# A two-layer graph transformer on one core: layer 0 gets its own order of token blocks, with the 20-token tile in its first block

## The chip, the cores and the metric

The kernel runs on one core of one Trainium2 chip. The metric is the time of one launch in device microseconds, as the median over several runs. A profile is taken from one execution of its own; its span runs from the first to the last instruction.

## The reference

Two layers of the same kind run one after the other over 2708 tokens of 512 features, in float32. A token attends only to its neighbours in a sparse graph (and itself), with 8 heads of 64.

```python
mask = adj.astype(jnp.float32) + jnp.eye(n, dtype=jnp.float32)
q = (h @ Wq.T + bq).reshape(n, N_HEADS, D_K)      # k and v alike
scores = jnp.einsum('nhd,mhd->hnm', q, k) / jnp.sqrt(jnp.float32(D_K))
scores = jnp.where(mask[None, :, :] == 0, jnp.float32(-1000000000.0), scores)
attn = jax.nn.softmax(scores, axis=-1)
ctx = jnp.einsum('hnm,mhd->nhd', attn, v).reshape(n, D_MODEL)
h1 = _layer_norm(h + ctx @ Wo.T + bo, ln1_g, ln1_b)
ff = jax.nn.relu(h1 @ W1.T + b1) @ W2.T + b2      # D_FF = 2048
h2 = _layer_norm(h1 + ff, ln2_g, ln2_b)
```

The graph is random: a pair of tokens is joined with a probability of some 0.003, so a token has 9 neighbours or so, and few have over 20.

## The kernel before, in words

**Tiles and lists.** The kernel first makes a list of neighbours for every token, sorts the tokens by their number of neighbours, and cuts the sorted row into 22 tiles (NT) of 128 tokens; the last, tile 21, has 20. `CAPS` (L37) gives the number of neighbours that a tile's tokens may have: 22 for tile 0, then 14, 13, 12, 12, 11, 11, 10, 10, 9, 9, 9, 9, 8, 8, 8, 7, 7, 7 for tiles 1 to 18, 6 and 5 for 19 and 20, and 3 for tile 21. Keys and values of all tokens lie in DRAM (`kv_d`), queries too (`q_d`); rows are gathered by index.

**Attention** (`attend`, L1759, class `Tile`, L1139) runs on VectorE and ScalarE. It takes a tile's neighbours in chunks of one or two (`SLOTS`). For a chunk, `weights` multiplies the gathered keys by the query and sums over each head on VectorE (L1150, L1156); `weigh` takes the exponential on ScalarE (L1169), weighs the values on ScalarE (L1176) and VectorE (L1182), and adds them up on VectorE (L1189). After a tile's last chunk, `sums` (L1193) forms the sums, and `divided` (L1215, L1220) writes the attended rows `cx` on ScalarE. `weigh` comes one step behind `weights`, `sums` two and `divided` three, so that the next tile's first chunks stand between a tile's last chunk and its cx. Gathers run three chunks ahead (`EARLY`) into five buffers (`KVB`).

**Blocks.** The rest of a layer goes by blocks of two tiles (L1754), eleven in all: `attended` (L1434) turns cx with four transposes (tp, L1293), projects it (o, L620; L615 for the 20-token tile, whose four parts of the sum run side by side on quarters of the array and are added by VectorE in L630), adds the input and normalizes; `feed_forward` (L1475) has for each of 16 slices f of 128 hidden features four matmuls of the first product (pf, L1523), a relu on ScalarE (ft, L1534) and the slice's part of the second product (a, L1496, L1511 for the 20-token tile); `keys_values` (L1709) makes keys and values for the next layer, inside the next block's f = 5 to 8.

**Seven products.** In layer 0, most pairs of full tiles use `feed_forward_by_seven` (L1613): two slices f and two tiles make a 2x2 product of blocks, which is done with seven matmuls of 128x256 (L1643) in place of four of 128x512, with sums of weights (forms) and sums of activations. The weights' sums are formed once, on VectorE, in block 1 (`form`, L1587) and stored in DRAM (`form_d`); each block fetches them again, 21 times 128 KB, into three places (`ask_forms`, L1605), on SP's queue. The places lie in the buffer of Wq (`prepared`, L1575). The last pair of slices, f = 14 and 15, stays ordinary (L1673, L1677). One form overwrites a piece of W2, and the last block in seven products loads it again (`form_back`). After the products, VectorE puts the parts together (L1695 to L1703).

**The order of the work** is written out by hand: each engine runs its instructions in the order of the program. The main loop (L1928) goes through the blocks and, inside, through f. After a slice's matmuls, `advance` (L1820) lets the attention go on by a number of steps that the paces (L51 to L61) give for this f; a step of two neighbours costs 1.0, and what is left over is kept, up to 1.5. `until` (L1832) takes as many steps as a tile's cx needs. Block k+1 is attended inside block k: in layer 0 its first tile at f = 10 and its second at f = 11 (12 and 13 in block 0).

**Before block 0**, in layer 0, `first_queries` (L990) makes all queries in order of tokens, and stores them. Since the stored queries are complete only at the end, the first three tiles of the order have queries of their own (`own`, L1022); the fourth tile's query is gathered from `q_d` once all are stored (`asked`, L1122). Block 0's tiles are attended and turned in between.

**The seam of the layers.** In layer 0's last block (L1997 to L2009), which is the 20-token tile with tile 0 and ordinary, the next layer's W1, W2, Wq and Wo come in on SP's queue, with the stored activations of the next layer's first eight tiles. Then the queries of layer 1 run (L2016 and L1887 to L1923), with the last block's keys and values in between; the attention of layer 1 begins when the last keys are stored.

Both layers have one order: (20, 19), (18, 17), (8, 9), (7, 10), (6, 11), (5, 12), (4, 13), (3, 14), (2, 15), (1, 16), (21, 0).

## Time and profile before

| | before |
|---|---|
| median of 3 runs | 1831.61 us (1830.18 to 1831.98) |
| the profiled execution: span | 1827.1 us |
| what lies around the span, against the median | 4.5 us |
| mean granted TensorE clock | 0.999 |
| layer 0, block 0 starts | 250.12 us |
| layer 0, block 1 starts | 314.95 us |
| layer 0, block 2 starts (seven products) | 393.74 us |
| layer 0, last block starts | 1003.91 us |
| layer 1, block 0 starts | 1142.47 us |

A page gives the busy time of each engine: PE is TensorE's matmuls, PEld its weight loads, DVE VectorE, ACT ScalarE, POOL GpSimd, and SP the queue that issues most loads. A timeline's row has the start, the length, the engine, the line, what is written <- what is read, the shape and the number of instructions that were merged (a float32 matmul shows as two records), and in brackets the idle time ahead of it with its releaser. The names are the program's: pf and ft are the first product and its relu, a and c the sums of the second product, tp a transpose, cx a tile's attended rows, o, q, k and v the projections.

### The profile page before, as it was taken

The numbers are of one execution on the slowest core, as the hardware profiler recorded it, in microseconds if no ns is written. First come the engines' busy times: TensorE is split into PE (matmuls) and PEld (weight loads), VectorE is DVE, ScalarE is ACT, GpSimd is POOL, SyncE is SP. The second block draws the span as 40 slices with busy tenths as digits, with TensorE's granted clock in tenths as the row PEclk, the third lists the DMA queues.
The fourth block names the chain that finished last, engine by engine and source line by source line (L and its number), as shares of the span: only waits on it lengthen the run. The fifth ranks groups of instructions, "written<-read, shape, count | busy, mean of one in ns | idle before, by whom it ended". The sixth has DMA issues, their size and how long they took to land.

```text
span 1827.1 us, 22528 instructions
## 1 busy us (share of the span) xinstructions
PE 1807.5 (99%) x6563; PEld 1162.6 (64%) x6563; DVE 1457.5 (80%) x2447; ACT 949.1 (52%) x3271; POOL 798.9 (44%) x745
## 2 busy tenths in 40 slices
PE   9999999999999999999999999999999999999998
PEld 4444456666777867778677644666666666666666
DVE  5887778988989889898895257887898888889853
ACT  5771435645556545564543213665665565567531
POOL 3334755534455544454430042353464555456302
PEclk9999999999999999999999999999999999999999
DMA  9997987757576676765652876745564664555300
GB/s 340 369 335 256 371 283 245 236 169 241 195 255 228 197 236 196 219 233 181 228 191 70 287 257 248 285 160 180 178 228 150 228 224 169 195 197 194 133 14 21
DMA packets 158061, 393.80 MB, mean 216 GB/s; under 512 B 17514, under 2 KB 60894, under 8 KB 157928
## 3 DMA queue, kind: packets, MB, share of 16 engines
q0 software_dynamic: 70608, 252.12, 40.2%
q1 hardware_dynamic: 77162, 118.55, 18.7%
q10 hardware_dynamic: 10158, 21.61, 3.1%
q8 instruction: 53, 0.87, 0.2%
q14 instruction: 80, 0.66, 0.1%
HBM read 338.78 MB, written 53.44 MB: 215 GB/s over the span
## 4 chain that ended last, share of the span: by engine, by line
PE 89%; DVE 5%; issue 2%; ACT 2%; DMA 1%; POOL 1%; POOLq 0%; SPq 0%; DVEq 0%
PE pf L1523 18%; PE a L1496 17%; PE pf L1653 9%; PE k L620 8%; PE v L620 8%; PE q L620 8%; PE o L620 8%; PE c L1643 4%; PE a L1643 3%; PE tp L1293 2%; DVE sc L1156 1%; DVE kv L1150 1%; DMA forms<-form_d 1%; PE a L1677 1%; PE a L1673 1%
## 5 line engine op out<-in xcount | busy, mean ns | idle before, releaser
L1113 POOL DMA_INDIRECT kv<-kv_d,listed x420 | 524.0, 1248 | 291.2 <-DVE acc L1189 133.9
L1523 PE MATMUL pf<-hT,w 128*128 128x256 f32 (+1 forms) x1792 | 393.2, 367 | 0.1
L1523 PEld LDWEIGHTS pf<-hT,w 128*128 128x128 f32 x1792 | 323.5, 190 | 103.1 <-issue 64.4
L1496 PE MATMUL a<-w,ft 128*128 128x512 f32 x800 | 373.1, 592 | 0.0
L1176 ACT ACTIVATE kv<-kv,p 128x64 f32<-128x64 f32 x1232 | 311.0, 335 | 5.0
L1275 POOL TENSOR_TENSOR rd<-va,mhalf 128x1 f32<-128x1 f32 (+1 forms) x88 | 80.5, 914 | 520.6 <-DVE va L1273 520.5
L1150 DVE TENSOR_TENSOR kv<-kv,q 128x1024 f32<-128x1024 f32 (+1 forms) x222 | 256.9, 1157 | 13.3 <-DMA q<-q_d,ident_i 10.9
L1156 DVE TENSOR_REDUCE sc<-kv 128x16 f32<-128x1024 f32 (+1 forms) x222 | 257.9, 1162 | 7.6
L1189 DVE TENSOR_TENSOR acc<-acc,kv 128x1024 f32<-128x1024 f32 (+2 forms) x178 | 205.4, 1154 | 37.6 <-ACT kv L1176 23.0
L1653 PE MATMUL pf<-hT,w 128*128 128x256 f32 x1024 | 233.1, 379 | 1.6 <-ACT ft L1664 1.6
L1496 PEld LDWEIGHTS a<-w,ft 128*128 128x128 f32 x800 | 150.1, 190 | 113.2 <-issue 101.3
L1653 PEld LDWEIGHTS pf<-hT,w 128*128 128x128 f32 x1024 | 193.9, 190 | 35.4 <-issue 7.9
L1534 ACT ACTIVATE ft<-pf,b 128x256 f32<-128x256 f32 (+1 forms) x208 | 95.0, 459 | 197.6 <-PE pf L1523 195.2
L1169 ACT ACTIVATE p<-sc,listed 128x8 f32<-128x8 f32 x420 | 104.0, 296 | 147.2 <-DVE sc L1156 135.7
L620 PE MATMUL o<-wo,cT 128*128 128x512 f32 x336 | 151.0, 593 | 1.0 <-ACT cT L1298 1.0
L1664 ACT ACTIVATE ft<-pf,b 128x256 f32<-128x256 f32 x96 | 44.9, 468 | 160.5 <-PE pf L1653 160.5
L1182 DVE TENSOR_TENSOR kv<-kv,p 128x512 f32<-128x512 f32 (+1 forms) x178 | 123.4, 693 | 4.5 <-ACT p L1169 4.3
L620 PEld LDWEIGHTS o<-wo,cT 128*128 128x128 f32 x336 | 63.4, 190 | 74.7 <-issue 65.5
L745 DVE MAX8 tops<-code 128x8 f32<-128x247 f32 (+2 forms) x242 | 78.6, 400 | 28.3 <-ACT code L740 28.3
L1281 DVE SCALAR_TENSOR_TENSOR h<-h,rd,ln_b 128x512 f32<-128x512 f32 (+1 forms) x88 | 65.9, 749 | 39.5 <-POOL rd L1275 39.5
L1220 ACT ACTIVATE cx<-acc,su 128x64 f32<-128x64 f32 (+1 forms) x352 | 88.2, 333 | 12.9 <-DVE su L1212 7.4
L1455 DVE TENSOR_TENSOR h<-o,xb 128x512 f32<-128x512 f32 (+1 forms) x44 | 30.3, 688 | 80.0 <-PE o L620 65.0
(232 smaller groups left out, 2323.5 us busy)
## 6 DMA issues: line engine op xcount, KB each, us to landing
aj<-in_adj SPq DMA_DIRECT2D x42, 677.0 KB, 6.3
forms<-form_d SPq DMA_DIRECT2D x168, 128.0 KB, 4.2
kv_d<-kvs ACTq DMA_DIRECT2D x21, 512.0 KB, 5.5
xg<-in_xT SPq DMA_DIRECT2D x19, 512.0 KB, 7.4
w<-in_W SPq DMA_DIRECT2D x16, 512.0 KB, 6.2
kv<-kv_d,listed POOLq DMA_INDIRECT x420, 6.3
zT_d<-zT SPq DMA_DIRECT2D x22, 256.0 KB, 5.1
xb_d<-h SPq DMA_DIRECT2D x21, 256.0 KB, 5.7
```

The source lines that it names most:

```text
L620: nc.tensor.matmul(o[:r], xs(c), wm[:, c, :], start=(c == 0), stop=(c == NC - 1))
L1113: return nc.gpsimd.indirect_dma_start(out=to, out_offset=None, in_=table[:, :], in_offset=bass.IndirectOffsetOnAxis(ap=s, axis=0), bounds_ ...
L1150: nc.vector.tensor_tensor(kv[:r, :c, :DM], kv[:r, :c, :DM], self.q[:r].unsqueeze(1).to_broadcast([r, c, DM]), ALU.mult,)
L1156: nc.vector.tensor_reduce(self.sc[:r, s0 : s0 + c, :], kv[:r, :c, :DM].rearrange("p s (h d) -> p s h d", d=DK), AX.X, ALU.add,)
L1169: nc.scalar.activation(p[:r, s, :], self.sc[:r, s, :], AF.Exp, bias=minus[:r, g, s : s + 1])
L1176: nc.scalar.activation(to[:, i, hd], kv[:r, i, DM + h * DK : DM + (h + 1) * DK], AF.Copy, scale=p[:r, s0 + i, h : h + 1],)
L1182: nc.vector.tensor_tensor(to[:, 0, :].rearrange("p (h d) -> p h d", d=DK), kv[:r, 0, DM:].rearrange("p (h d) -> p h d", d=DK), p[:r, s0, : ...
L1189: nc.vector.tensor_tensor(self.acc[:r, :c, :], self.acc[:r, :c, :], kv[:r, :c, DM:], ALU.add)
L1496: nc.tensor.matmul(a[:r, cols], fts[f][:, c0 : c0 + r], self.w2[f // 2][:, f % 2, cols], start=(f == 0), stop=(f == NFC - 1),)
L1523: nc.tensor.matmul(pf[:, :w], self.w1[f // 2][:, c, f % 2 * P : f % 2 * P + P], hT[:, c, :w], start=(c == 0), stop=(c == NC - 1),)
L1643: nc.tensor.matmul(to, left, right, start=start, stop=stop)
L1653: nc.tensor.matmul(pf[:, :W], self.w1[j][:, c, f % 2 * P : f % 2 * P + P], hT[:, c, :], start=(c == 0), stop=(c == NC - 1),)
```

## The change

Each layer gets its own plan of blocks. Layer 1 keeps the order that it had. In layer 0 the 20-token tile (NT - 1 = 21) goes to block 0, with tile 20, and the last block is (16, 15). The neighbours of the blocks are 11, 14, 19, 19, 20, 20, 20, 20, 21, 21, 25 before, and 8, 13, 20, 20, 20, 21, 21, 21, 29, 22, 15 after.

Block 0 is then the ordinary block of 148 tokens, block 1, in which the forms are made, the only ordinary pair of full tiles, and all blocks from 2 to the last use seven products: nine in place of eight. In the last block the forms' places lie in a buffer of keys (`prepared(apart=True)`), because Wq of layer 1 comes into theirs. W2 isn't needed whole again, so `form_back` goes. W2 of layer 1 is loaded two slices of f later, its parts 5 and 6 after the last keys. At the seam, three queries stand ahead of the last block's turns and one between these and the keys, where there was one ahead of the first turn and one behind it, and four of the eight loaded tiles are left for the queries behind the keys, where there were six. The paces of the attention are changed: in layer 0's block 0 from 0.85 and 0.8 to 0.7, in block 1 up by 0.05, in the blocks of seven products from 0.6 to 0.75 at f = 9 and 10.

```diff
--- before.py
+++ after.py
@@ -49,14 +49,14 @@
 LISTS = (4, 7, 9, 12, 13, 14, 15, 17, 18, 19)
 EARLY = 3
 PACES = (
-    (0.0,) * 4 + (0.85,) * 8 + (0.0,) * 2 + (0.8,) * 2,
+    (0.0,) * 4 + (0.7,) * 8 + (0.0,) * 2 + (0.7,) * 2,
     (0.75,) * 11 + (0.0,) * 2 + (0.9,) * 3,
 )
-PACE7 = (0.0,) * 4 + (0.6,) + (1.3,) * 4 + (0.6,) * 2 + (0.0,) * 2 + (0.5, 0.8, 2.4)
+PACE7 = (0.0,) * 4 + (0.6,) + (1.3,) * 4 + (0.75,) * 2 + (0.0,) * 2 + (0.5, 0.8, 2.4)
 FORMED = 1
 FORMS = (3, 5, 7, 9, 11, 13, 15)
 PACE = (
-    (0.0,) * 2 + (0.6,) * 3 + (1.2,) * 4 + (0.6,) * 2 + (0.0,) * 2 + (0.8,) * 3,
+    (0.0,) * 2 + (0.65,) * 3 + (1.25,) * 4 + (0.65,) * 2 + (0.0,) * 2 + (0.85,) * 3,
     (0.0,) * 2 + (0.82,) * 9 + (0.0,) * 2 + (1.0,) * 3,
 )
 
@@ -1572,17 +1572,21 @@
                 zs.append(z)
             yield zs
 
-        def prepared(self):
-
-            place = wts.tile([P, NC, DM], F32, tag="wq", name="forms")
-            place = place.rearrange("p c n -> p (c n)")
+        def prepared(self, apart=False):
+
+            if apart:
+                place = at.tile([P, SLOTS, 2 * DM], F32, tag="kv", name="forms", bufs=KVB)
+                place = place.rearrange("p s n -> p (s n)")
+            else:
+                place = wts.tile([P, NC, DM], F32, tag="wq", name="forms")
+                place = place.rearrange("p c n -> p (c n)")
+                self.asked = 0
             W = 2 * P
             self.slots = [place[:, i * W : (i + 1) * W] for i in range(3)]
             sums = place[:, 3 * W : 6 * W].rearrange("p (two s t) -> p two s t", two=2, t=P)
             self.sums = [sums[:, i] for i in range(2)]
             self.other_slots = [place[:, i * W : (i + 1) * W] for i in range(3, 6)]
             self.more_fts = [place[:, i * W : (i + 1) * W] for i in (6, 7)]
-            self.asked = 0
 
         def form(self, j):
 
@@ -1595,12 +1599,6 @@
             nc.vector.tensor_tensor(t4, b21, t2, ALU.subtract)
             for i, t in enumerate((t2, t3, t4)):
                 nc.sync.dma_start(out=form_d[j, i], in_=t)
-
-        def form_back(self, j):
-            W = 2 * P
-            nc.sync.dma_start(
-                out=self.w2[j][:, 0, W:], in_=chunked(self.w["W2"])[:, 2 * j, W:]
-            )
 
         def ask_forms(self, upto):
 
@@ -1642,8 +1640,6 @@
                 ):
                     nc.tensor.matmul(to, left, right, start=start, stop=stop)
                 self.ask_forms(base + min(3 * j + 6, 3 * J + 3 * (k < NB - 2)))
-                if k == NB - 2:
-                    self.form_back(j)
 
             self.ask_forms(base + 3)
             for f in range(NFC):
@@ -1722,8 +1718,7 @@
                 zTs.append(zT)
 
             turn(0)
-            if block != blocks[-1]:
-                turn(1)
+            turn(1)
             yield
             for i, (g, z) in enumerate(zip(block, zs)):
                 r, zT = size(g), zTs[i]
@@ -1731,8 +1726,6 @@
                 k = project(lambda c: zT[:, c, :r], r, self.kv[0], "k")
                 nc.vector.tensor_tensor(kv[:r, :DM], k[:r], self.bk[:r], ALU.add)
                 plus_rest(kv[:r, :DM], k, r)
-                if len(zTs) == 1:
-                    turn(1)
                 v = project(lambda c: zT[:, c, :r], r, self.kv[1], "v")
                 nc.scalar.copy(kv[:r, DM:], v[:r])
                 plus_rest(kv[:r, DM:], v, r)
@@ -1751,10 +1744,15 @@
     now = Layer(0, layers[0])
 
 
-    blocks = [(20, 19), (18, 17), (8, 9), (7, 10), (6, 11), (5, 12)]
-    blocks += [(4, 13), (3, 14), (2, 15), (1, 16), (NT - 1, 0)]
+    plans = [
+        [(20, NT - 1), (19, 18), (7, 8), (6, 9), (5, 10), (4, 11)]
+        + [(3, 12), (2, 13), (17, 0), (1, 14), (16, 15)],
+        [(20, 19), (18, 17), (8, 9), (7, 10), (6, 11), (5, 12)]
+        + [(4, 13), (3, 14), (2, 15), (1, 16), (NT - 1, 0)],
+    ]
+    orders = [[g for block in plan for g in block] for plan in plans]
+    blocks, order = plans[0], orders[0]
     NB = len(blocks)
-    order = [g for block in blocks for g in block]
 
     def attend(n, got):
 
@@ -1786,7 +1784,7 @@
                 t.weights(kv, s0, c)
                 if q is None and g != order[-1]:
                     q, later = later or asked(n, order[order.index(g) + 1]), None
-                if g == order[-3] and i == 2:
+                if g == order[-3] and i == 2 and size(order[-2]) <= Q4:
                     later = asked(n, order[-1])
                 done.append((t, kv, s0, c, last))
             else:
@@ -1892,7 +1890,7 @@
             next(streamed)
             now.stores = nc.scalar
             while pool:
-                if len(pool) < 5:
+                if len(pool) < 3:
                     advance(0.65)
                 now.query(*pool.pop(0))
             for i, _ in enumerate(streamed):
@@ -1931,11 +1929,11 @@
                 asking = iter(())
             if n > 0 and 0 < k < NB - AHEAD:
                 asking = now.queries(blocks[k + AHEAD])
-            seven = n == 0 and FORMED < k < NB - 1
-            if n == 0 and k == FORMED:
-                now.prepared()
-            if n == 0 and k in (FORMED + 1, NB - 1):
-                places_of_psum(3 - seven, seven)
+            seven = n == 0 and FORMED < k
+            if n == 0 and k in (FORMED, NB - 1):
+                now.prepared(k > FORMED)
+            if n == 0 and k == FORMED + 1:
+                places_of_psum(2, True)
             if seven:
                 working = now.feed_forward_by_seven(k, block, hs, hT)
             else:
@@ -1997,8 +1995,8 @@
                 if not last and not more:
                     if f % 2:
                         nxt.load_w1(f // 2)
-                        if f > 2:
-                            nxt.load_w2(f // 2 - 1)
+                        if f > 6:
+                            nxt.load_w2(f // 2 - 3)
                     if f == 6:
                         nxt.load_first()
                         nxt.load_second(0, temp)
@@ -2006,21 +2004,25 @@
                         nxt.settle()
                     if f == 7:
                         finish(ahead)
-                        pool += nxt.preloaded(order[:8], temp)
+                        pool += nxt.preloaded(orders[n + 1][:8], temp)
             if not last:
                 behind = now.keys_values(block, zs)
             if more:
                 hs = hs_next
         if not last:
+            places_of_psum(3)
+            blocks, order = plans[n + 1], orders[n + 1]
             nxt.wq = now.wq
-            for _ in range(2):
+            for _ in range(3):
                 nxt.query(*pool.pop(0))
-                if len(pool) % 2:
-                    next(behind)
+            next(behind)
+            nxt.query(*pool.pop(0))
             nxt.kept()
             for g in order[:2]:
                 own[g] = asked(n + 1, g)
             finish(behind)
+            for j in (5, 6):
+                nxt.load_w2(j)
             behind = None
             now = nxt
     return again
```

## The prediction

> **What bounds the kernel.** I read the page's head, then TensorE's waits, then the stages in windows, then the timelines of the stretches that the change touches.
>
> ```profile
> span 1827.1 us, 22528 instructions
> ...
> PE 1807.5 (99%) x6563; PEld 1162.6 (64%) x6563; DVE 1457.5 (80%) x2447; ACT 949.1 (52%) x3271; POOL 798.9 (44%) x745
> ```
> ```profile
> PE o L615 <- ACT cT L1298: 2.4, 1, 2.4
> ```
> TensorE is busy for 99% of the span, and no single wait of it is longer than this one of 2.4 us (after the row's sum come the count and the longest). So removed matmul time counts in full, and so does every new wait: TensorE takes its work in the written order, and nothing fills a hole. What VectorE has left decides whether there are holes:
>
> ```profile
> 250.10:318.00 67.90, 67.26 (x239) 43.62 (x240) 50.02 (x65) 36.53 (x135) 34.46 (x31) 1.00 0.77 261
> 318.00:393.70 75.70, 75.70 (x253) 45.76 (x252) 66.06 (x101) 42.08 (x158) 38.11 (x32) 1.00 0.68 222
> 849.00:926.00 77.00, 77.00 (x319) 58.14 (x318) 69.26 (x118) 44.12 (x166) 37.36 (x31) 1.00 0.61 201
> ```
> The windows are block 0, block 1 and a late block in seven products; after the window's length come TensorE's, the weight loads', then VectorE's busy time. Attention is VectorE's work, and VectorE needs 66 of 76 us in block 1 and 69 of 77 in the late one, the norms and sums among them. A block that gets shorter has no room for it.
>
> **The matmuls.** Prices are the distances between starts, since ends are modelled:
>
> ```profile
> 257.14 1.88 PE L1496 MATMUL a<-w,ft 128*128 128x512 f32 x4
> 258.85 1.89 PE L1523 MATMUL pf<-hT,w 128*128 128x256 f32 x8
> 260.58 1.88 PE L1496 MATMUL a<-w,ft 128*128 128x512 f32 x4
> ...
> 692.85 1.88 PE L1673 MATMUL a<-w,ft 128*128 128x512 f32 x4
> 694.57 1.89 PE L1677 MATMUL a<-w,ft 128*128 128x256 f32 x8
> 696.29 0.59 PE L1643 MATMUL a<-forms,ft 128*128 128x256 f32 x2
> ...
> 710.55 0.60 PE L1643 MATMUL a<-forms,ft 128*128 128x256 f32 x2
> ...
> 713.57 1.89 PE L1653 MATMUL pf<-hT,w 128*128 128x256 f32 x8
> ```
> One f of an ordinary pair's second product takes 1.71 us, 16 of them 27.4. In seven products, one j takes 713.57 - 710.55 = 3.02, seven of them 21.1, and the two groups left over 1.72 each: 24.6. Before, layer 0 has two ordinary pairs of full tiles, eight pairs in seven products and one block of 148 tokens; after, one, nine and one. So one block goes from 27.4 to 24.6: **-2.8 us**. Every other matmul is only moved.
>
> The 148-token block moves from the end to block 0. Its prices, from where it runs now:
>
> ```profile
> 1008.88 1.05 PE L1511 MATMUL a<-w,ft 128*20 128x512 f32 x8
> 1009.87 1.27 PE L1523 MATMUL pf<-hT,w 128*128 128x148 f32 x8
> 1010.98 1.02 PE L1496 MATMUL a<-w,ft 128*128 128x512 f32 x2
> 1011.84 1.17 PE L1523 MATMUL pf<-hT,w 128*128 128x148 f32 x8
> 1012.85 1.02 PE L1496 MATMUL a<-w,ft 128*128 128x512 f32 x2
> ```
> That is 1.01 for a group of the first product, 0.86 of the second, 0.99 for four quarters. The 2.4 us for which o L615 waited go with it: in block 0 both tiles are turned ahead, among queries. **-2.4 us**; nothing else of the 20-token tile was late.
>
> **The first deadlines.** Only three tiles have their queries of their own (`own`, order[:3]); the fourth waits for q_d, which is complete only after the last query. Before, the fourth is tile 17; after, 18, which has as many neighbours (7).
>
> ```profile
> 250.08 3.22 SPq L1010 DMA_DIRECT2D q_d<-qs  x2
> ```
> ```profile
> 258.54 1.01 POOL L1113 DMA_INDIRECT q<-q_d,ident_i  x1 [4.28 <-issue]
> ```
> ```profile
> 250.12 7.17 PE L1523 MATMUL pf<-hT,w 128*128 128x256 f32 x32
> ...
> 293.89 3.60 PE L620 MATMUL o<-wo,cT 128*128 128x512 f32 x8
> 297.33 0.60 PE L1293 MATMUL tp<-ident,cx 128*128 128x128 f32 x4
> 297.76 1.89 PE L1523 MATMUL pf<-hT,w 128*128 128x256 f32 x8
> ...
> 370.07 0.60 PE L1293 MATMUL tp<-ident,cx 128*128 128x128 f32 x4
> ```
> ```profile
> 263.87 1.23 DVE L1150 TENSOR_TENSOR kv<-kv,q 128x1024 f32<-128x1024 f32 x1 [10.90 <-DMA q<-q_d,ident_i]
> ...
> 355.09 0.20 DVE L1212 RECIPROCAL su<-su 128x8 f32<-128x8 f32 x1
> ```
> ```profile
> 287.93 2.01 ACT L1220 ACTIVATE cx<-acc,su 128x64 f32<-128x64 f32 x8
> ...
> 358.35 2.00 ACT L1220 ACTIVATE cx<-acc,su 128x64 f32<-128x64 f32 x8
> ```
> Count from the start of block 0 (250.12). The stores of the last queries, the gather behind them and VectorE's wait of 10.9 us put the fourth tile's first product at 13.75. Its cx is done at 289.94, which is 39.8, and TensorE turns it at 297.33, which is 47.2: 7.4 us to spare. The change leaves that chain alone: the last query, its store, the gather, seven neighbours. But TensorE now arrives after 14 groups of 1.01, 11 of 0.86, three of 0.99, one turn (0.43, from 297.33 to 297.76) and one o (3.44, from 293.89): 30.4. **It stands still for 9.4 us.** ScalarE gives that wait in parts, since relu's evictions stand behind the attention's activations in its queue, and they behind VectorE.
>
> The deadline of block 1's last turn (tile 9 before, 8 after) is worse. Before: at 370.07, which is 120.0, with cx done at 360.35 (110.2). After, TensorE's work to that point is block 0 whole, 16 x 1.01 + 16 x 0.86 + 4 x 0.99 + 2 x 3.44 + 4 x 0.43 = 42.5, and of block 1 12 x 1.73 + 9 x 1.71, keys and values of one full tile (6.9, two at o's price) and of 20 rows (2 x 0.99), three turns (1.3) and an o: 49.7. Together 92.2, that is 27.8 earlier. What VectorE does meanwhile:
>
> ```profile
> 263.87:355.30 91.43, 90.81 (x308) 55.67 (x307) 81.29 (x114) 53.16 (x201) 47.76 (x39) 1.00 0.70 229
> ```
> ```profile
> L1150 DVE TENSOR_TENSOR kv<-kv,q 128x1024 f32<-128x1024 f32 (+1 forms) x222 | 256.9, 1157 | 13.3 <-DMA q<-q_d,ident_i 10.9
> ```
> ```profile
> 1063.73 2.13 DVE L630 TENSOR_TENSOR kvs<-k,kvs 20x512 f32<-20x512 f32 x3
> ```
> It is busy for 81.3 of 91.4 us. After, the same tiles' places hold 7, 10 and 10 neighbours instead of 7, 10 and 9: one neighbour more, half of three operations of about 1.16, 1.7 us. The 20-token tile adds its three times three partial sums (output, key, value), 3 x 2.13 = 6.4. So 89.4 busy at least; of the 10.1 idle I keep 2.5, for the norms' short waits and ScalarE's. The sums of tile 8 are then done at 13.75 + 92 = 105.7, and cx 5.05 later (355.29 to 360.35): 110.8. TensorE waits 110.8 - 92.2 = **+18.6 us** in all, the 9.4 being part of it. Ends: without any idle time, and only cx's own 2.0 behind it, +13; with all idle time kept, +26. A lead gathered earlier can't help, since the fourth tile cannot start before its query; the change even moves four neighbours (11 to 7) out of blocks whose attention is done before that. In block 2 VectorE and TensorE go about evenly, so I add nothing (0 to +4). Later pairs are nearly as heavy as before; the 29 neighbours of (17, 0) stand in front of 22 and 15, and the last blocks have room.
>
> **The seam of the layers.**
>
> ```profile
> 1071.77 17.33 PE L620 MATMUL q<-wq,zTs 128*128 128x512 f32 x40
> ...
> 1120.12 0.60 PE L1293 MATMUL tp<-ident,cx 128*128 128x128 f32 x4
> ...
> 1123.99 0.60 PE L1293 MATMUL tp<-ident,cx 128*128 128x128 f32 x4
> ```
> ```profile
> 1121.26 1.76 ACT L1220 ACTIVATE cx<-acc,su 128x64 f32<-128x64 f32 x7
> ```
> Layer 1's attention starts from the last keys. Before, two queries stand ahead of them and 14 (each at o's price of 3.44) between them and the first turn; after, four and 12. The second tile's cx comes at 1123.02, 51.3 after the keys; TensorE now wants it after 12 queries, a turn and a query, 45.2. It would be 6.1 late; VectorE has two evictions fewer in between, so **+5** (0 to +8). The cover of the new, longer chain of sums after the last block is the three queries ahead of the turns, 10.3 us.
>
> **The last block's forms.** They now share SP's queue with W1, W2, Wo and the stored activations of the next layer, and a late form stops TensorE.
>
> ```profile
> forms<-form_d SPq DMA_DIRECT2D x168, 128.0 KB, 4.2
> ```
> A form is fetched again while 2 x 1.73 + 3.02 - 0.43 = 6.05 us pass, and lands in 4.2. Two loads ahead of it take most of the margin: +0.5 (0 to +10, six refills by 1.7). Nothing else of the edit is on the path: the place of the forms is a free buffer of keys, and dropping form_back takes seven small loads out.
>
> **Sum.** All this is against one execution with a span of 1827.1; the median of the runs is 1831.6, 4.5 more, and I let that stand. 1831.6 - 2.8 - 2.4 + 18.6 + 5 + 0.5 = **1850.5 us**, 1.0% slower. Its own range is 1839 (13 for the waits and nothing else) to 1861 (26, 8 at the seam and 0.5); all upper ends at once I don't expect.
>
> **The clock.** A stop may cost more than its length:
>
> ```profile
> 4.93 5.04 PE L620 MATMUL k<-wk,xg 128*128 128x512 f32 x8
> 9.80 3.60 PE L620 MATMUL v<-wv,xg 128*128 128x512 f32 x8
> ```
> The first product of the kernel took 5.04, the next alike one 3.60: 1.4 us lost by a start from rest. [...]
>
> **Rivals.** (1) TensorE stays fed, because the fourth tile's query comes earlier or VectorE has more in hand than I count: then only the removed work is left, 1831.6 - 2.8 - 2.4 = 1826.4, faster. Against it stand the 10.9 us of VectorE's wait and the 7.4 us of spare time against 16.8 us of earlier arrival; the point at which it decides is a query in hand 9.4 us sooner, and 18.6 us less work for VectorE by block 1's last turn. Chance 0.13. (2) The waits come to some 5 us and cancel the gain: within 0.2%, 0.07. (3) Only the first deadline costs, and VectorE then uses idle time that I think bound: 1826.4 + 9.4 plus 0 to 5 at the seam, 1836 to 1841, 0.10. (4) The forms queue behind the layer's loads at every j: 1860, 0.05. (5) The array runs slow after each long stop; stops within VectorE's stretch hide it, the last one and the seam's don't: 2 x 1.4 more, 1853, 0.05. My forecast has 0.60.
>
> **Numbers.** A measurement of this kernel tells about 0.2% (3.7 us) from no change. Faster 0.13, the same 0.07, slower 0.80. The range takes in (3), (4) and (5) and leaves out (1) and (2): 1835 to 1863.
>
> **What would show it.** In the profile after: TensorE's waits on ScalarE's ft and cT, or as turns behind cx, sum to 15 to 26 us between the start of block 0 and the end of block 1, and VectorE is over 90% busy there; VectorE still waits for q<-q_d after the last query; a wait of some 5 us at the second turn of layer 1; L1643 has nine blocks of 98 records (882 in place of 784). Wrong would be a TensorE at 99% with block 0 in 43 us, or waits that name the forms.

## The result, and the profile after

The kernel after the change takes 1913.07 us (1906.93 to 1915.14, median of 4 runs) beside 1831.53 us (1830.18 to 1831.98, 4 runs) for the kernel before on the same chip: the ratio is 1.044, with a 95% interval of 1.0427 to 1.0454. Forecast were 1850.5 us, 1835 to 1863. The direction was right; the loss is 81.5 us instead of 18.9.

The page of the profile after, its head, the busy times, and TensorE's clock in 40 slices:

```profile
span 1913.2 us, 22691 instructions
...
PE 1838.1 (96%) x6609; PEld 1181.4 (62%) x6609; DVE 1471.3 (77%) x2484; ACT 954.3 (50%) x3272; POOL 798.1 (42%) x745
...
PEclk9999988999999999998999999999999999999999
```

TensorE went from 99% to 96%. In three slices the clock shows an 8, and the mean granted clock fell from 0.999 to 0.982. VectorE is busy for 14 us more than before and idle for 72 us more. So the time is neither in more work nor in a fuller VectorE; it points to an order in which the two wait for each other.

Block by block, here blocks 0 to 4, 6, 7 and 9 of layer 0, and the last block with the seam behind it (columns as in the windows of before; the clock stands after POOL's column):

```profile
247.40:315.70 68.30, 55.34 (x228) 30.88 (x224) 43.66 (x58) 33.79 (x129) 30.23 (x27) 0.85 0.69 227
315.70:395.30 79.60, 75.63 (x272) 45.32 (x269) 74.68 (x111) 43.66 (x164) 38.52 (x33) 1.00 0.62 200
395.30:475.70 80.40, 76.80 (x312) 56.69 (x311) 70.04 (x115) 42.39 (x158) 38.85 (x32) 1.00 0.66 219
475.70:557.50 81.80, 78.38 (x312) 57.69 (x311) 68.40 (x113) 42.38 (x157) 36.62 (x31) 0.96 0.62 208
557.50:644.10 86.60, 80.53 (x312) 59.38 (x311) 72.10 (x116) 44.29 (x165) 41.27 (x33) 0.94 0.63 207
...
724.90:801.00 76.10, 75.82 (x311) 56.60 (x311) 69.01 (x117) 44.55 (x168) 37.11 (x33) 1.00 0.69 236
801.00:895.20 94.20, 81.73 (x312) 59.19 (x312) 82.53 (x121) 50.51 (x190) 45.53 (x37) 0.93 0.64 210
...
981.40:1057.60 76.20, 75.66 (x311) 56.74 (x311) 34.62 (x79) 23.05 (x76) 8.27 (x8) 1.00 0.22 72
1057.60:1228.40 170.80, 163.18 (x514) 94.44 (x513) 74.77 (x137) 37.52 (x129) 34.41 (x32) 0.99 0.65 230
```

Block 0 was meant to become 22 us shorter; it takes 68.3 us where it took 64.8. Block 7, which attends tile 0, takes 94.2; only blocks 6 and 9 have the length of before, 76.1 and 76.2. In block 9 VectorE is busy for only 34.6: its unused time lies behind the last heavy tile, where nobody needs it. All of layer 1 is as long as before.

TensorE's waits from block 0 to the seam (sum, count, longest):

```profile
PE o L620 <- ACT cT L1298: 15.4, 6, 3.4
PE tp L1293 <- DVE h L1281: 11.9, 9, 2.2
PE tp L1293 <- ACT cx L1220: 9.3, 2, 8.6
PE a L1511 <- ACT ft L1534: 5.9, 2, 3.4
PE o L620 <- ACT forms L1660: 5.0, 2, 4.0
PE a L1511 <- ACT cx L1220: 4.8, 1, 4.8
PE q L620 <- DMA zT<-zT_d: 4.0, 2, 3.2
```

Attended rows that were not there (cx) are the smaller part; most waits are for evictions (cT, ft, forms) and norms (h), small steps that the written order puts behind steps of the attention on ScalarE and VectorE (one such place is shown at experiment 12).

In the table, a stop is time without a running matmul, and "half" is half of the time at a granted clock of 0.5 in which TensorE was not stopped, an estimate of what the lower clock cost. Both are worked out from the instructions and clock records of each profile, in us, from the first matmul to the last; each pair is stops + half. Each ratio is to before on the same chip, and the medians of before lie between 1827.6 and 1831.5 us, so small gains are read from the ratios. One slow run each of experiments 8 and 13 (3894.4 and 8329.8 us) is left out of their medians and ratios.

| kernel | median us | ratio (95% interval) | before block 0 | blocks 0, 1 | blocks 2 to 9 | last block and seam |
|---|---|---|---|---|---|---|
| before | 1831.5 | 1 | 0.2 + 0 | 0.6 + 0 | 6.3 + 0 | 0.9 + 0 |
| after | 1913.1 | 1.0440 (1.0427 to 1.0454) | 2.4 + 0 | 16.9 + 7.5 | 36.6 + 17.0 | 7.6 + 1.6 |
| 1 order alone | 1908.3 | 1.0430 (1.0413 to 1.0447) | 2.3 + 0 | 19.2 + 7.2 | 44.4 + 9.8 | 0 + 0 |
| 2 fourth query | 1887.5 | 1.0321 (1.0304 to 1.0338) | 10.4 + 0 | 16.1 + 7.1 | 17.0 + 3.4 | 7.4 + 1.7 |
| 3 light pair first | 1884.9 | 1.0311 (1.0294 to 1.0329) | 3.2 + 0 | 18.6 + 10.1 | 18.8 + 1.4 | 6.9 + 1.7 |
| 4 all paces up | 1912.4 | 1.0454 (1.0432 to 1.0476) | 2.3 + 0 | 28.7 + 11.6 | 28.3 + 6.7 | 6.7 + 3.0 |
| 5 before, two own queries | 1840.4 | 1.0051 (1.0033 to 1.0069) | 0.2 + 0 | 3.3 + 1.7 | 13.5 + 3.4 | 0.9 + 0 |
| 6 cover back | 1918.4 | 1.0471 (1.0449 to 1.0493) | 2.4 + 0 | 5.3 + 1.7 | 36.6 + 17.1 | 6.5 + 1.7 |
| 7 stops filled | 1910.6 | 1.0438 (1.0416 to 1.0459) | 2.4 + 0 | 15.2 + 5.8 | 24.0 + 6.1 | 6.6 + 0 |
| 8 seam's loads later | 1909.7 | 1.0440 (1.0416 to 1.0464) | 2.3 + 0 | 16.5 + 7.5 | 38.0 + 7.6 | 6.7 + 0 |
| 9 cover and lead | 1892.5 | 1.0358 (1.0340 to 1.0375) | 2.5 + 0 | 13.6 + 7.4 | 13.0 + 1.4 | 5.5 + 1.7 |
| 10 lead alone | 1890.7 | 1.0352 (1.0335 to 1.0369) | 2.4 + 0 | 29.6 + 12.7 | 12.1 + 0 | 6.5 + 1.4 |
| 11 second and third | 1899.5 | 1.0391 (1.0374 to 1.0409) | 9.6 + 0 | 21.1 + 9.7 | 22.4 + 6.0 | 6.7 + 0 |
| 12 no step ahead of turns | 1914.4 | 1.0465 (1.0448 to 1.0483) | 2.4 + 0 | 17.4 + 7.5 | 44.6 + 10.1 | 7.0 + 2.8 |
| 13 the same, with lead | 1920.6 | 1.0503 (1.0482 to 1.0524) | 2.4 + 0 | 30.7 + 12.1 | 29.8 + 10.9 | 5.2 + 1.7 |

From before to after, the stops of the whole span grow by 55.4 us (9.1 to 64.5) and the half clock by 26.1 (0 to 26.1). With 4.6 for all the rest, the products' gain among it, that is the 86.1 us between the spans.

### The profile page after: what moved, and what is told of

It is laid out like the page before. It is cut to its first block, busy times and chain, and to the rows that moved or that the text cites. A ratio compares the mean times of both kernels' runs of the same rounds, so it can differ in the third digit from the quotient of the medians.

```text
span 1913.2 us, 22691 instructions
## 1 busy us (share of the span) xinstructions
PE 1838.1 (96%) x6609; PEld 1181.4 (62%) x6609; DVE 1471.3 (77%) x2484; ACT 954.3 (50%) x3272; POOL 798.1 (42%) x745
## 4 chain that ended last, share of the span: by engine, by line
PE 73%; DVE 14%; ACT 4%; issue 4%; DMA 2%; POOL 1%; DVEq 0%; POOLq 0%; ACTq 0%; SPq 0%
PE pf L1523 14%; PE a L1496 14%; PE o L620 7%; PE k L620 7%; PE v L620 7%; PE pf L1649 6%; PE q L620 6%; PE c L1641 3%; DVE sc L1156 3%; DVE kv L1150 3%; PE a L1641 3%; ACT kv L1176 2%; PE tp L1293 2%; DVE acc L1189 2%; DVE kv L1182 1%
## 5 line engine op out<-in xcount | busy, mean ns | idle before, releaser
L1523 PE MATMUL pf<-hT,w 128*128 128x256 f32 (+1 forms) x1664 | 365.8, 368 | 0.0
L1496 PE MATMUL a<-w,ft 128*128 128x512 f32 x736 | 346.3, 596 | 0.7 <-DVE h L630 0.7
L1150 DVE TENSOR_TENSOR kv<-kv,q 128x1024 f32<-128x1024 f32 (+2 forms) x222 | 256.8, 1157 | 12.8 <-DMA q<-q_d,ident_i 10.4
L1156 DVE TENSOR_REDUCE sc<-kv 128x16 f32<-128x1024 f32 (+2 forms) x222 | 258.0, 1162 | 7.6
L1649 PE MATMUL pf<-hT,w 128*128 128x256 f32 x1152 | 261.5, 379 | 0.0
L1189 DVE TENSOR_TENSOR acc<-acc,kv 128x1024 f32<-128x1024 f32 (+1 forms) x178 | 205.4, 1154 | 36.5 <-ACT kv L1176 21.1
L1496 PEld LDWEIGHTS a<-w,ft 128*128 128x128 f32 x736 | 139.0, 191 | 104.8 <-issue 92.0
L1169 ACT ACTIVATE p<-sc,listed 128x8 f32<-128x8 f32 (+1 forms) x420 | 104.2, 296 | 176.4 <-DVE sc L1156 159.3
L620 PE MATMUL o<-wo,cT 128*128 128x512 f32 x336 | 161.2, 626 | 21.5 <-ACT cT L1298 16.4
L1182 DVE TENSOR_TENSOR kv<-kv,p 128x512 f32<-128x512 f32 x178 | 123.6, 694 | 10.6 <-ACT p L1169 9.6
```

The lines of the kernel that those rows point to most:

```text
L620: nc.tensor.matmul(o[:r], xs(c), wm[:, c, :], start=(c == 0), stop=(c == NC - 1))
L1150: nc.vector.tensor_tensor(kv[:r, :c, :DM], kv[:r, :c, :DM], self.q[:r].unsqueeze(1).to_broadcast([r, c, DM]), ALU.mult,)
L1156: nc.vector.tensor_reduce(self.sc[:r, s0 : s0 + c, :], kv[:r, :c, :DM].rearrange("p s (h d) -> p s h d", d=DK), AX.X, ALU.add,)
L1169: nc.scalar.activation(p[:r, s, :], self.sc[:r, s, :], AF.Exp, bias=minus[:r, g, s : s + 1])
L1182: nc.vector.tensor_tensor(to[:, 0, :].rearrange("p (h d) -> p h d", d=DK), kv[:r, 0, DM:].rearrange("p (h d) -> p h d", d=DK), p[:r, s0, : ...
L1189: nc.vector.tensor_tensor(self.acc[:r, :c, :], self.acc[:r, :c, :], kv[:r, :c, DM:], ALU.add)
```

## The experiments

**1. The order alone.** The kernel before with only layer 0's new order; its paces and its seam stay, and the last block stays ordinary.

```diff
-    blocks = [(20, 19), (18, 17), (8, 9), ..., (1, 16), (NT - 1, 0)]
+    plans = [[(20, NT - 1), (19, 18), (7, 8), ..., (1, 14), (16, 15)], (the old order)]
```

> The kernel before with nothing but layer 0's new order of blocks: its paces, its eight blocks in seven products and its seam stay, and the last block (16, 15) is an ordinary pair. Theory A (the order takes cover from the attention in block 0, and layer 0 never gets it back) expects the whole loss and the 2.8 us that the ninth block in seven products saves: 1905 to 1925 us. The rival B (the last block in seven products, its forms and the seam cost the time) expects 1830 to 1840.

Measured: 1908.3 us. The order holds the whole loss; what else the change does can't be told from nothing here. Its seam, with the queries placed as before, has no stop at all.

**2. A query of its own for the fourth tile** (tile 18), made before block 0 like the first three.

```diff
+                own[order[3]] = temp()
...
+            if t == OWN + 2:
+                xrs.append(own_rows(order[3]))
...
+            if t == OWN + 7:
+                zTs = [turned_own(order[3], xrs[3])]
+            if t == OWN + 8:
+                own_query(order[3], zTs[0], to[order[3]], bq, wq)
```

> The changed kernel, but tile 18, the fourth of the order, gets a query of its own as the first three have, for one more projection of 3.4 us and a turn of 0.4. Theory A1 (the late fourth query starts the loss, and VectorE has no time to make it good) expects the stops of blocks 0 and 1 to go, some 25 to 30 us with their half clock, and the rest in blocks 2 to 8 to stay: 1875 to 1890. Theory A2 (the attention's steps merely stand too late in the written order, and three steps of lead are enough) expects nearly all stops before block 7 to go: 1835 to 1855. If the query isn't the cause: 1915 to 1918.

Measured: 1887.5 us, some 22 less than after by the ratios. The time lies in the range of A1, but by luck: the gain is hardly where the query was late (blocks 0 and 1: from 24.4 to 23.2, and 8.0 more stops come before block 0), but in blocks 2 to 9, from 53.6 to 20.4. What the query buys is lead: the attention's steps are written two or three chunks further ahead, up to tile 0.

**3. Light tiles first.** (17, 16) becomes the third pair, (15, 0) the last.

```diff
-        [(20, NT - 1), (19, 18), (7, 8), (6, 9), (5, 10), (4, 11)]
-        + [(3, 12), (2, 13), (17, 0), (1, 14), (16, 15)],
+        [(20, NT - 1), (19, 18), (17, 16), (7, 8), (6, 9), (5, 10)]
+        + [(4, 11), (3, 12), (2, 13), (1, 14), (15, 0)],
```

> The changed kernel with (17, 16) as block 2 and (15, 0) as the last, so that from block 2 on six neighbours fewer are due at each deadline and the heavy tile 0 is due last; everything else is as changed. The stop in block 0 stays in any theory (about 15 us with its half clock). Theories A1 and A2 expect the stops of blocks 2 to 8 to go for the most part: 1850 to 1870. The rival B expects no change: 1910 to 1916.

Measured: 1884.9 us. The side was right, the gain too small: blocks 2 to 9 fall to 20.2, blocks 0 and 1 rise by 4.3.

**4. All paces of layer 0 up.**

```diff
-    (0.0,) * 4 + (0.7,) * 8 + (0.0,) * 2 + (0.7,) * 2,
+    (0.0,) * 4 + (0.85,) * 8 + (0.0,) * 2 + (1.2,) * 2,
...
-PACE7 = (0.0,) * 4 + (0.6,) + (1.3,) * 4 + (0.75,) * 2 + (0.0,) * 2 + (0.5, 0.8, 2.4)
+PACE7 = (0.0,) * 4 + (0.8,) + (1.5,) * 4 + (0.9,) * 2 + (0.0,) * 2 + (0.8, 1.0, 2.4)
...
-    (0.0,) * 2 + (0.65,) * 3 + (1.25,) * 4 + (0.65,) * 2 + (0.0,) * 2 + (0.85,) * 3,
+    (0.0,) * 2 + (0.85,) * 3 + (1.5,) * 4 + (0.85,) * 2 + (0.0,) * 2 + (1.1,) * 3,
```

> The changed kernel with the paces of the attention raised: 0.85 and 1.2 in block 0, 0.85, 1.5 and 1.1 in block 1, 0.8, 1.5, 0.9, 0.8 and 1.0 in the blocks of seven products; no work is added or removed, the steps of the attention only stand earlier in the written order, by some four steps at block 2's second turn. Theory A1 (VectorE has no time) expects no gain: 1905 to 1925. Theory A2 (the steps stand too late) expects the stops from block 2 on to go: 1850 to 1870.

Measured: 1912.4 us, no gain. The waits move from the later blocks into blocks 0 to 2: blocks 3 to 9 fall from 50.0 us (stops and half clock) to 23.4, blocks 0 to 2 rise from 28.0 to 52.0. I took this for the proof that lead can't be written; the tenth run shows that it was too early.

**5. The kernel before with one own query less.** The third tile, 18, has to wait for the stored queries, and TensorE has 3.9 us less to do.

```diff
-                for g in order[:3]:
+                for g in order[:2]:
...
-                xrs.append(own_rows(order[2]))
...
-            if t == OWN + 5:
-                zTs = [turned_own(order[2], xrs[2])]
-            if t == OWN + 6:
-                own_query(order[2], zTs[0], to[order[2]], bq, wq)
```

> The kernel before with only two own queries in place of three: the third tile of its order, 18, now has to wait for the stored queries too, and TensorE has one query less to make (3.4 us of matmuls and 0.4 of a turn, -3.9). Theory A (in this kernel VectorE's attention steps ahead of block 0 are needed later, so a query that comes late is a debt that TensorE pays in stops, each with some time at half clock): 1835 to 1845 us, slower than before although there is less to compute; some 8 us of VectorE's steps are lost, and block 0 with its 64.8 us of TensorE work cannot cover them all. Theory B (the late query is covered in this order; what fails after the change is not the lateness of a query): 1825 to 1827, the 3.9 us saved.

Measured: 1840.4 us, 1.0051 (1.0033 to 1.0069) of the time before, with less work. Only 5.0 us come in block 0; the largest part, 11.1, comes in block 9, nine blocks behind the cause, at tile 0's turn: steps that aren't written at the start are missing until the end.

**6. Cover put back.** Two empty products of 128x512 for each f of block 0, which the real ones overwrite.

```diff
             for f in range(NFC):
                 pf = ps_f.tile([P, DM], F32, tag="f", name="pf")
+                for _ in range(2 if self.n == 0 and block == blocks[0] else 0):
+                    nc.tensor.matmul(pf, ident, self.wo[:, 0, :], start=True, stop=True)
```

> The changed kernel with empty TensorE work in layer 0's block 0: two products of 128x512 more for each of the 16 slices, written into pf ahead of its real products, which overwrite them; 32 x 0.86 = 27.5 us. Theory A (block 0 has lost 22 us of cover, and the later stops are that debt): the time does not rise by 27.5 but falls, to 1865 to 1905; stops in layer 0 fall from some 57 us to under 25, half clock likewise. Theory B (the stops of blocks 3 to 8 come from their own weights of neighbours, whatever block 0 does): 1935 to 1942, the whole 27.5 on top.

Measured: 1918.4 us, between the two. Block 0 goes from 68.3 to 72.1 us although 27.5 us of work are in it, so the cover is nearly free there. But from block 2 on nothing changes. Its blocks 2, 3 and 4 in windows:

```profile
401.00:481.40 80.40, 76.80 (x311) 56.63 (x310) 69.98 (x115) 42.49 (x158) 38.79 (x32) 1.00 0.66 219
481.40:563.20 81.80, 78.44 (x312) 57.62 (x311) 68.37 (x113) 42.23 (x157) 36.62 (x31) 0.96 0.62 208
563.20:649.80 86.60, 80.55 (x312) 59.33 (x311) 72.06 (x116) 44.37 (x165) 40.94 (x33) 0.94 0.63 208
```

These are the lengths of the same blocks of after, to a tenth of a us. VectorE did nothing with the cover; its longest wait in this block 0 is this one, in the timeline:

```profile
302.97 0.69 DVE L1455 TENSOR_TENSOR h<-o,xb 128x512 f32<-128x512 f32 x1 [12.05 <-PE o L620]
```

It had done all steps that were written there and stood ahead of the norm, which needs TensorE's o. My theory that TensorE pays later for cover missing in block 0 falls here: a longer block 0 doesn't help later ones, because VectorE goes by the written order too.

**7. Stops filled.** Three empty products (2.6 us) ahead of the first tile's o in blocks 1 to 10.

```diff
                 g, r, cT = cTs[i]
+                if self.n == 0 and i == 0 and block != blocks[0]:
+                    fill = ps.tile([P, DM], F32, tag="g", name="fill")
+                    for _ in range(3):
+                        nc.tensor.matmul(fill, ident, self.wo[:, 0, :], start=True, stop=True)
```

> The changed kernel with three empty products of 128x512 (2.6 us) ahead of the first tile's output projection in blocks 1 to 10 of layer 0. TensorE there often stops for the turned rows by 2 to 3.4 us, and the half clock follows behind such stops. If the stops' lengths alone cost (theory C: half clock is hidden behind VectorE): the empty work adds up to 10 x 2.6 = 26 us less what it takes of 16.4 us of stops, so 1913 to 1925. If the half clock costs its own 28.5 us (theory A): filled stops keep the clock up, and the time comes to 1895 to 1910 although work is added.

Measured: 1910.6 us, between the two cases, and its interval overlaps that of after: by time alone it decides nothing. In its profile the stops fall by 15.3 (64.5 to 49.2) and the half clock by 14.2 (26.1 to 11.9; the 28.5 of the expectation takes in time at half clock behind the last matmul, which costs nothing), while some 23 of work are added. With 23 us more work its span is still 6.7 us shorter (1906.5 beside 1913.2); filling 15.3 us of stops saved some 30.

**8. Seam's loads later.** Parts 5 and 6 of layer 1's W2 come just before layer 1's block 0.

```diff
-            now.load_w2(NFC // 2 - 1)
+            for j in (5, 6, 7):
+                now.load_w2(j)
...
-            for j in (5, 6):
-                nxt.load_w2(j)
```

> The changed kernel with parts 5 and 6 of layer 1's W2 loaded just before layer 1's block 0, with part 7, instead of at the seam, where they stand in SP's queue ahead of the loads of stored activations for which TensorE waits 4.0 us. If these loads cause the stops at the seam (7.6 us of stops and 1.6 of half clock there): 1904 to 1908. If the stops come from the two queries that no longer stand ahead of the turns: 1910 to 1915, no change. A third outcome, slower, if the loads then come too late for layer 1's block 0 (up to 1925).

Measured: a ratio of 1.044, as after. TensorE still waits 4.5 us for the stored activations, so these two loads are not the cause. In experiment 1 the seam has no stop; there the queries stand as before, but W2's other loads too (the change puts its parts four slices of f later, not two), and the last block is ordinary. So the new order of the queries is likely and not shown, and why it would make these activations late I didn't try.

Its profile shows something else. Up to the seam it is the program of after, its stops sum to 64.6 us beside 64.5, and yet its span is 1901.3, 11.9 shorter. The half clock takes 15.1 instead of 26.1, which is some 11 of these 11.9. The same wait in block 3 in both timelines, after and then this kernel:

```profile
524.08 6.39 PE L620 MATMUL o<-wo,cT 128*128 128x512 f32 x8 [3.42 <-ACT cT L1298]
```
```profile
522.84 3.70 PE L620 MATMUL o<-wo,cT 128*128 128x512 f32 x8 [3.42 <-ACT cT L1298]
```

After 3.42 us of idle time the same eight matmuls take 6.39 us in one execution and 3.70 in the other. The last section shows the clock around both.

**9 and 10. Lead with cover, lead alone.** Block 0's paces go from 0.7 to 1.3, so that six more steps are written into it; in 9 with the empty products of experiment 6, in 10 without.

```diff
-    (0.0,) * 4 + (0.7,) * 8 + (0.0,) * 2 + (0.7,) * 2,
+    (0.0,) * 4 + (1.3,) * 8 + (0.0,) * 2 + (1.3,) * 2,
```

> The changed kernel with the same 27.5 us of empty TensorE work in layer 0's block 0, and besides with the paces of block 0 raised from 0.7 to 1.3, so that six more steps of the attention (a step is two neighbours, some 4 us of VectorE) are written into block 0. With the cover alone, the stops of blocks 2 to 8 stayed as they were to a tenth of a us, since VectorE, too, goes by the written order. Theory A (the lead in the written order is what keeps blocks 2 to 8 fed, and block 0's cover is what it takes to have it): stops and half clock in blocks 2 to 8, 36.1 + 17.0 us, fall to under 20, and the time comes to 1870 to 1895, well below the kernel with the cover alone. Theory B (blocks 2 to 8 hold too many neighbours each, a lead makes no difference): 1912 to 1922, as with the cover alone.

> The changed kernel with block 0's paces raised from 0.7 to 1.3 and no empty work: the lead without the cover. Theory A: the six steps are then waited for in blocks 0 and 1, whose stops and half clock (17.0 and 7.5 us) grow by some 20 to 30, and blocks 2 to 8 lose about as much: 1900 to 1918, no real gain. Theory C (the lead by itself is all that was missing, VectorE has the time anyway): 1865 to 1890.

Measured: 1892.5 with cover, 1890.7 without. The lead alone gains 16 us by the ratios, more than theory A allowed and just short of theory C. Number 9 came out as theory A had it, but number 10 shows that the lead doesn't need the cover. Its blocks 0, 2 and 3 in windows:

```profile
247.20:329.00 81.80, 59.09 (x228) 30.64 (x224) 64.50 (x81) 47.70 (x187) 45.27 (x38) 0.81 0.78 258
...
413.50:490.20 76.70, 75.69 (x311) 56.61 (x310) 66.96 (x112) 40.61 (x151) 37.56 (x31) 1.00 0.68 223
490.20:565.70 75.50, 75.50 (x312) 56.80 (x311) 68.65 (x113) 43.03 (x160) 38.41 (x32) 1.00 0.68 225
```

VectorE does 64.5 us of work in block 0 instead of 43.7, for 13.5 us more length. Then block 3 runs in 75.5 us without a stop, where after took 81.8, though VectorE has as many instructions in it (113) and as much to do (68.7 and 68.4 us). Blocks 2 to 9 fall from 53.6 to 12.1, and blocks 0 and 1 rise by 17.9. So VectorE can feed such a block, if it begins it ahead. The cover then pays in blocks 0 and 1, from 42.3 back to 21.0, about what it costs: 9 and 10 take the same time, though 9 does 24 us more work (1843.6 beside 1820.0 without stops and half clock).

**11. The second and third experiment together.** The edits are the two shown above.

> The changed kernel with both remedies that gained by themselves: the pair (17, 16) third and (15, 0) last (1.0311 of the time before alone), and a query of its own for the fourth tile (1.0321 alone). If they repay different stops: 1831.5 + 83 - 26 - 28 = 1858 to 1866. If they repay the same lead twice: 1875 to 1885. The kernel before stays faster in both cases, since the stops of block 0 and of the seam (some 15 and 9 us) are touched by neither.

Measured: 1899.5 us, worse than each alone and outside both expectations. Of its waits between blocks 1 and 10, 23.9 us in seven are o for cT, where experiment 3 had 6.3 and experiment 2 had 12.8. Why two leads together cost more than either is left open.

**12 and 13. Where in the block the steps stand.** No steps at f = 9 and 10, just ahead of the turns, and more at f = 3 to 8; in 12 alone, in 13 with the lead of 10. The reason was this piece of ScalarE's queue in the profile after, ahead of the wait of 3.42 us shown above:

```profile
518.96 0.49 ACT L1169 ACTIVATE p<-sc,listed 128x8 f32<-128x8 f32 x2 [2.04 <-DVE sc L1156]
519.48 2.02 ACT L1176 ACTIVATE kv<-kv,p 128x64 f32<-128x64 f32 x8
521.41 2.00 ACT L1220 ACTIVATE cx<-acc,su 128x64 f32<-128x64 f32 x8
523.32 0.45 ACT L1660 ACTIVATE forms<-pf,b 128x256 f32<-128x256 f32 x1
523.67 1.11 ACT L1298 ACTIVATE cT<-tp,bv 128x128 f32<-128x128 f32 x4
```

TensorE had turned these rows at 518.33; their eviction, cT, comes at 523.67, because an exponential ahead of it waits for VectorE, and a weighting and the next tile's cx follow.

```diff
-PACE7 = (0.0,) * 4 + (0.6,) + (1.3,) * 4 + (0.75,) * 2 + (0.0,) * 2 + (0.5, 0.8, 2.4)
+PACE7 = (0.0,) * 3 + (0.6,) * 2 + (1.5,) * 4 + (0.0,) * 4 + (0.5, 0.8, 2.4)
```

> The changed kernel with the paces of the blocks in seven products moved away from the turns: none at f = 9 and 10 (0.75 each before), the same sum at f = 3 to 8. In the trace of the changed kernel TensorE's longest common wait is o for cT, the ScalarE eviction of turned rows that had been ready 14 us and more; ScalarE holds it behind the exponential and the weighting of an attention step written at f = 9, which wait for VectorE. Theory D (the place of that step in ScalarE's queue is the cause in blocks 2 to 6): their stops and half clock, 16.8 + 8.9 us, fall to under 8, block 7 costs 2 to 5 more (two more forced steps at tile 0), and the time comes to 1895 to 1905. Theory A (VectorE is behind the written order by more than a step, wherever the step is written, for want of lead): 1908 to 1918, the stops only change their names.

> The same paces for the blocks in seven products, together with block 0's paces at 1.3 (the lead that alone gave 1890.7 us). With the lead, blocks 2 to 8 have only 12 us of stops left. Theory D: 4 to 8 us of these go, 1883 to 1888. Theory A: the lead has already taken what there was, 1888 to 1896.

Measured: 1914.4 us, as theory A had it, and 1920.6 us, above both ranges. The idea that this place in the queue is the cause falls. The wait of o for cT does shrink, but another takes over, in the waits of 12 from block 1 on:

```profile
PE pf L1649 <- ACT ft L1660: 18.4, 5, 4.9
PE tp L1293 <- ACT cx L1220: 17.0, 1, 17.0
...
PE o L620 <- ACT cT L1298: 2.7, 1, 2.7
```

Steps packed closer at f = 5 to 8 hold up the relus instead. And 13 is 28 us slower than 10 (by the ratios) with the same lead: it seems that lead helps only if the steps also stay evenly spread.

## Why the prediction was right on the side and wrong in size

**The first deadlines (+18.6)**: near in sum, partly by luck. The chain that it counted runs nearly to plan. VectorE waits 10.44 us for the fourth tile's query, and its first cx is done 40.1 us after block 0's start (39.8 were forecast). Up to that tile's turn TensorE stops for 2.49, 4.84 and 3.44 us, 10.8 instead of 9.4. Blocks 0 and 1 together have 16.9 us of stops, where the 18.6 stood; but block 0 has 13.0 of them, and block 1 only 4.0 where 9.2 were forecast. (The first three tiles hold 18 neighbours before and 14 after, not 11 and 7; the difference of four is right.) And "of the 10.1 idle I keep 2.5" and "over 90% busy" failed for block 0: VectorE is busy for 43.7 of 68.3 us there, and besides the query's wait it stands still for another 10.57:

```profile
260.78 1.22 DVE L1150 TENSOR_TENSOR kv<-kv,q 128x1024 f32<-128x1024 f32 x1 [10.44 <-DMA q<-q_d,ident_i]
...
299.68 0.69 DVE L1455 TENSOR_TENSOR h<-o,xb 128x512 f32<-128x512 f32 x1 [10.57 <-PE o L620]
```

TensorE, delayed by the stops and slow behind them, now makes VectorE wait in turn, because no further steps are written ahead of the norm. So block 1's last cx comes 124.4 us after block 0's start, not 110.8. TensorE comes later by as much, so the stops didn't grow with it, but 7.5 us of half clock came on top.

**Blocks 2 on**: the step that failed. "In block 2 VectorE and TensorE go about evenly, so I add nothing (0 to +4). ... the 29 neighbours of (17, 0) stand in front of 22 and 15, and the last blocks have room." Measured: 36.6 us of stops and 17.0 of half clock in blocks 2 to 9, where before had 6.3. It compared each block's VectorE time with its length, and asked only whether a block could bear its own load. What it left out is how far the written steps stand ahead of TensorE when a block begins. Counted in the order in which each kernel's code writes its steps, after has three or four chunks of later tiles in hand at each second turn up to tile 0's (three is the least, since a cx is written three steps behind its tile's last chunk), and before has four or five. At tile 0 three steps are missing in after, which are then forced at its turn (the wait of 8.6 us for cx above). The 29 neighbours do stand in front of light tiles, but their room comes behind them: VectorE is busy for 34.6 of 76.2 us in block 9.

Run 10, with eight or nine chunks in hand until tile 0, takes 41.5 of the 53.6 us of blocks 2 to 9 away, and pays 17.9 for it in blocks 0 and 1. In blocks 3 to 9 stops and half clock sum to 42 to 50 us where the new order has three or four chunks in hand (after, 1, 6, 8 and 12; 7, with its filled stops, is left aside), and to 11 to 30 where it has mostly five or more (2, 3, 4, 9, 10, 11 and 13). So these blocks lacked attention written ahead, and writing it ahead takes most of their loss away. But the count of chunks isn't the whole account. Runs 4, 11 and 13 have about as many in hand as run 10 and keep 23 to 30 us where it keeps 11. And experiment 5 has only three all along, in the old order, and loses 5.7 us in blocks 2 to 8, where after loses 53.0. VectorE has 469.6 us of work in these seven blocks in experiment 5, 501.7 in after and 480.5 in run 10, since steps written earlier also leave less to do later. How much of the 53.6 us is due to the lead and how much to the load, the runs don't separate.

**The clock**: the second step that failed. It was a rival at 0.05 with two stops at 1.4 us and "stops within VectorE's stretch hide it". It takes 26.1 us in twelve stretches, 24.5 of it in blocks 0 to 9, within VectorE's stretch; before has no half clock up to its last matmul. That this time is paid and not hidden is borne out by the executions of after and of experiment 8: nearly the same stops, some 11 us less lost at half clock, a span 11.9 shorter.

**The seam (+5, 0 to +8)**: size near, mechanism wrong. Stops and half clock are 8.3 above before's. The forecast wait at the second turn is 0.7 us; the largest part, 4.0, are queries that wait for stored activations, which I hadn't priced, though four loaded tiles were left for them instead of six.

**The products (-2.8), the removed wait (-2.4), the forms (+0.5)**: L1641 (L1643 before) has 882 matmul records as foretold, o no longer waits in a 20-token form (L615), and TensorE waits 1.0 us for forms. The rivals "fed" and "the same" are out, and so is the one of the forms; "only the first deadline costs" failed on the same step as the forecast.

Against the forecast's terms: the blocks 2 to 9 give 47.3 more than nothing (53.6 - 6.3), the half clock of blocks 0 and 1 7.5, the seam 3.3. These three are 58.1 of the 62.6 us that were missing; the rest, 4.5, isn't placed.

No version in this order beat the kernel before. The best, experiment 3, takes 1.0311 (1.0294 to 1.0329) of its time: blocks 0 and 1 alone hold 28.7 us of stops and half clock in it, and the ninth block in seven products was to give 2.8 us.

## What to carry to other kernels

Where several engines run one written order, ask of a reordering not only whether each stage can bear its load, but how many steps the slower engine is ahead when the stage begins; here a lead lost at the start was missing in later stages, and neither spare time at the end nor a longer stage brought it back unless the steps were written into it. Price a stop of TensorE at more than its length: here 64.5 us of stops came with 26.1 us lost at half clock. And when a remedy fails (paces up everywhere), try it in one place before dropping its idea.

## What the runs showed of the hardware

The twelve half-clock stretches that after's clock records show up to its last matmul begin at whole multiples of 3.413 us from each other (from 266.7 to 522.7 us are 75 of them, to 1198.5 are 273) and last one, two or three. On this grid, from 200 to 1800 us of after's span, all eleven stretches at full clock with 2.04 us of idle time of TensorE or more were followed by one at half clock, as was one with 1.82; none with 1.78 or less was. In one of the eleven, from 905.0 us, the idle time isn't in one go: it is a stop of 1.17 us and the first 0.89 of another, 2.06 in all. The clock came back only behind stretches with 0.58 us of idle time or less, though one with 0.31 stayed slow.

Here are the stretches around the 3.42 us stop of block 3, after first and then the kernel of experiment 8 (TensorE's busy time behind the length, the clock third from the end):

```profile
519.30:522.71 3.41, 1.36 (x7) 0.85 (x5) 3.34 (x7) 3.38 (x15) 2.79 (x3) 1.00 1.01 345
522.71:526.13 3.42, 2.05 (x3) 1.02 (x4) 3.18 (x7) 2.44 (x9) 2.64 (x2) 0.50 0.96 341
```
```profile
517.82:521.23 3.41, 1.60 (x8) 1.07 (x6) 3.15 (x7) 3.38 (x15) 2.80 (x3) 1.00 1.01 386
521.23:524.65 3.42, 1.81 (x4) 0.87 (x5) 3.28 (x6) 2.67 (x10) 2.81 (x3) 1.00 0.95 345
```

The first row of each has 3.41 - 1.36 = 2.05 and 3.41 - 1.60 = 1.81 us of idle time. After the first the clock is 0.50, after the second it stays at 1.00, and the rest of the stop (1.37 and 1.61) lies in the second row. So the same stop of 3.42 us brought half clock in one execution and not in the other, with 0.24 us less of its idle time in the first row. The 1.81 us here, without half clock behind them, and the 1.82 in after, with it, are nearly the same, so these two executions don't show where the border lies. After's four runs scatter over 8.2 us, the two longest at a mean granted clock of 0.982 and the shortest at 0.986; before's scatter over 1.8. That the place of the stops on this grid makes after's scatter is my estimate and not shown.
